# Grouped v weights, later decay exponentials, first tile by sequences, and a moved weight sum in a linear attention kernel with routed gate

## The chip, the cores and the metric

The kernel runs on one core of one Trainium2 chip. Times are device microseconds (us) of one execution. The kernel before took 1069.27 us (median of 3 runs, 1067.15 to 1069.29). Engines: PE = TensorE (matrix products), DVE = VectorE, ACT = ScalarE, POOL = GpSimd, SP = SyncE, which issues most DMAs; ACT issues some too.

## The reference

Input x has 4 sequences of 512 tokens and 512 features. With a layer norm, a linear attention of 16 heads of 128 with a decay for each head, and a gate that a router of 64 experts makes from their bias vectors:

```
xn = layernorm(x)
q, k, v = split(silu(xn @ w_qkv.T))                  # 16 heads of 128
o[t] = sum over s <= t of exp(-slope * (t - s)) * (q[t] . k[s]) * v[s]    # computed by blocks
o = norm_w * o * rsqrt(mean(o * o) + 1e-6)
s = (sigmoid(xn @ w_gate.T) * o) @ w_out.T
p, idx = top_k(softmax(xn @ router_w.T + router_b), 8)
g = silu(xn * sum(p) + sum over the 8 of p * expert_bias[idx])
out = x + s * g
```

## The kernel before, in words

**Products.** Every fp32 product is made of three fp32r passes: each operand is split into a high part, which ACT casts (split_hi, L100), and a low part, the rest, which DVE or POOL subtracts (split_lo, L103). Projections treat two sequences (a pair) as a 2x2 block matrix: the x blocks B11, T1, B21, B22 and the sums T2 to T4 on one side, the weight blocks A11, A12, A21, A22 and the sums S1 to S4 on the other. unit (L484) makes the result from 7 block products (PRODUCTS), each of 6 matmuls; plain_unit (L525) uses 8 and needs no sums. Each list after[i] in the code holds what is emitted after product i: work for other units, queued on its engine there.

**Stage v** (L939 to 1004). 16 units: for each of two groups of v weights (ws[0], ws[1]) the 8 tiles of 128 tokens x 2 sequences. The first two units (k = 0 and 1) are plain; in them DVE makes the four sums of the weights (sum_of, L421) and the S blocks are split, so that the third unit can use unit. Each unit also prepares a later tile: layer norm statistics (layer_norms, L221: DVE, with the power -1/2 on POOL, L232 or L236), normalising (L202, DVE), transposes (L251, PE) and their copy (L253, ACT), router logits (L318, PE), token sums (L268, POOL) and splits. Results go to DRAM (v<-vo_v, L588). A result's silu is a sigmoid on ACT (L555) and a product on DVE (L558), which is deferred to a later do_deferred; the product frees the PSUM bank. There are four such banks (ps_mm) and three of another pool (ps_sc), which transposes, logits and attention share.

**Start** (L892 to 937). SP issues x of the first two tiles and the eight pieces of the first v weights, each 128 rows of two runs of 1 KB (raw_v, L418). ACT's queue issues five small loads (L900 to 904). make_dist (POOL) and make_decays (ACT exponentials, then a memset on POOL, L169) build the decay rows. PE runs 32 transposes of the identity (warm_up, L150), then the first tile's transposes of both sequences, 6 more of the identity, logits and the first products.

**Decays.** keep_rows (L172) stores the 16 decay rows to DRAM; keep_decay(h) (L175) copies one row to 128 rows in DRAM, 16 DMAs on SP's queue in units 13 to 15 of stage v; load_decay (L655) reads it for head h. The router's exponentials (scores_exp, L337) run in unit 13, with a load of ACT's exponential table before and of the sigmoid's after.

**Head stage** (L1039 to 1095). For each of the two pairs 24 units: gates g and heads qk, three units to two heads. While a unit's products run, the attention of the head before it goes on PE: scores sa and transposed keys kt (scores_qk, L670), states ss, outputs o (attend, L707). The decay masks the scores on DVE (L680), which frees sa's bank of ps_sc; ACT scales the keys (L684) and POOL the queries (L686). y goes to DRAM.

**Output stage** (L1112 to 1155). For each sequence b and head h, o_head (L816) adds 12 matmuls into four banks. ahead(i, loads, splits) (L1015) loads y and w_o and splits them some heads ahead: y's low part on DVE, w_o's on POOL. The last unit of the head stage calls ahead in its after lists. The last head's attention is emitted in steps 0 to 2 of this stage. finish (L808) makes the result of a token tile and stores it, on SP's queue for the first three sequences.

Nothing reorders what is emitted: each engine works its instructions off in the order of the code, and a waiting one holds up those behind it.

Of the kernel before, what the change touches and what calls it, by code (L numbers as in the profile page):

```python
# [16 lines left out]
GH = 2  # L17
# [2 lines left out]
TOP_K = 8  # L20
LN_EPS = 1e-05
RMS_EPS = 1e-06
WARM = 32

# [24 lines left out]
def kernel(  # L51
# [44 lines left out]
    def tok(b, t):  # L96
        return bass.ds(b * N + t * P, P)

    def split_hi(hi, src):
        nc.scalar.copy(hi, src)  # L100

    def split_lo(eng, lo, src, hi):
        eng.tensor_tensor(lo, src, hi.bitcast(F32), ALU.subtract)  # L103
# [68 lines left out]
        nc.sync.dma_start(out=rows_d, in_=decay_row)  # L172

    def keep_decay(h):
        nc.sync.dma_start(out=decay_d[h], in_=rows_d[h : h + 1].to_broadcast([P, W]))  # L175


    stats = [const.tile([P, NT, 2], F32, tag=f"stats{b}", name=f"stats{b}") for b in range(B)]
# [39 lines left out]
        xts[b, t] = xt  # L218


    def layer_norms(p, t, apart=False):  # L221
        var = small.tile([P, PB], F32, tag="lnvar", name=f"lnv_{p}_{t}")
        for j in range(PB):
            b = p * PB + j
            st = small.tile([P, nc.vector.BN_STATS_DIM], F32, tag="bn", name=f"bn_{b}_{t}")
            nc.vector.bn_stats(st, xts[b, t])
            nc.vector.bn_aggr(stats[b][:, t, :], st)
            nc.vector.tensor_scalar(
                var[:, j : j + 1], stats[b][:, t, 1:2], 1.0, LN_EPS, ALU.mult, ALU.add
            )  # L230
            if apart:
                nc.gpsimd.tensor_tensor(  # L232
                    rstd_of[p][:, t, j : j + 1], var[:, j : j + 1], mhalf[:, 0:1], ALU.pow
                )
        if not apart:
            nc.gpsimd.tensor_tensor(rstd_of[p][:, t], var, mhalf[:, 0:PB], ALU.pow)  # L236

    def normalise_x(p, t):
        for b in range(p * PB, p * PB + PB):
# [94 lines left out]
            top = scores[p, "top"][:, :, None].to_broadcast([P, PB * NT, E])  # L334
            nc.vector.tensor_tensor(sc, sc, top, ALU.subtract)

    def scores_exp():  # L337
        for p in range(B // PB):
            nc.scalar.activation(scores[p], scores[p], AF.Exp)
        for b in range(B):  # L340
            nc.sync.dma_start(out=scores_d[b], in_=scores[b // PB][:, b % PB])

# [59 lines left out]
    class Weights:  # L402
# [38 lines left out]
            self.of[n] = self.wp.tile([P, 2, self.width], F32R, tag="w", name=f"w_{n}_{self.name}")  # L441


        def split_one(self, n, eng, piece=None, hi=False):
            src = self.sum[int(n[1]) - 1] if n[0] == "S" else self.raw[:, int(n[1]) - 1, int(n[2]) - 1]
            if n not in self.of:
                self.place(n)

            for i in (0, 1) if piece is None else (piece,):
                c = bass.ts(i, self.width // 2)  # L450
                if hi:
                    split_hi(self.of[n][:, 0, c], src[:, c])
                elif i == 0:
                    split_hi(self.of[n][:, 0], src)
                split_lo(eng, self.of[n][:, 1, c], src[:, c], self.of[n][:, 0, c])

        def splits(self, lo_engines):
            w, r, s, wp = self.width, self.raw, self.whole, self.wp
# [108 lines left out]

    def v_weights(p, g, rawp, sump, wp):
        def loads(raw):
            r = raw.rearrange("p i k (c w) -> p i k c w", c=KC)  # L570
            per = VH // GH
            return [
                (r[:, i, k, :, bass.ts(j, GH * P)], w_v[(2 * g + i) * per + j][:, bass.ts(k, KC)])
                for i in range(2) for k in range(2) for j in range(per)
            ]
        return Weights(f"v_{p}_{g}", KC * VW, rawp, sump, wp, loads, True)

    def v_unit(p, g, t, w, outp, after, direct=False):
        name = f"v_{p}_{g}_{t}"

        def operands(wn, xn, wi, xi, c):
            return blocks[p, xn][:, t, xi, c], w.of[wn][:, wi, bass.ts(c, VW)]

        def sink(i, j):
            dst = outp.tile([P, VW], F32, tag="vout", name=f"vo{i}{j}_{name}")

            def store():
                nc.sync.dma_start(out=v_d[p * PB + j, 2 * g + i][t], in_=dst)  # L588
            return dst, lambda src: silu_of(dst, src, f"{i}{j}_{name}", store)

        if direct:
            plain_unit(name, operands, lambda i, j, ps: sink(i, j)[1](ps), after)
            return
        unit(
            name, operands, lambda ps: sink(0, 0)[1](ps),
            [lambda: sink(1, 1), lambda: sink(0, 1), lambda: sink(1, 0)], after,
        )
# [202 lines left out]
    def split_wo(h, w):  # L800
# [3 lines left out]
        split_lo(nc.gpsimd, wr[:, 1], w, wr[:, 0])  # L804
        wos[h] = wr


    def finish(b, t, ps, c=slice(None)):  # L808
        u, xt = gates[b, t][:, c], xts[b, t][:, c]
        last = b == B - 1  # L810
        nc.vector.scalar_tensor_tensor(u, ps[:, c], rms[b][:, t : t + 1], u, ALU.mult, ALU.mult)  # L811
        (nc.vector if last else nc.gpsimd).tensor_tensor(u, u, xt, ALU.add)
        (nc.scalar if last and t % 2 else nc.sync).dma_start(out=out[tok(b, t), c], in_=u)


    def o_head(pos, h, yr, t, c=slice(None), stops=(NH - 1,)):  # L816
# [10 lines left out]
    NP_FIRST = 2  # L827

    def prepare(stage, p, t):
        first = (p, t) == (0, 0)  # L830

        def turn():
            for j in range(PB):
                transpose(stage, p, j, t)
            if p == 0:
                nc.sync.dma_start(out=xf_d[t], in_=xfs[p, t])

        if p == 0 and t < NP_FIRST:
            sums = (lambda: plain(p, t, nc.vector if t == 0 else nc.gpsimd)), lambda: None, lambda: None
        else:  # L840
            sums = combine(stage, p, t, nc.gpsimd)

        def route_logits():
            logits(stage, p, t)
        return {
            "stats": lambda: layer_norms(p, t, first), "norms": lambda: normalise_x(p, t),
            "turn": turn, "sums": sums[0], "plain": sums[1], "more": sums[2], "logits": route_logits,
        }

# [46 lines left out]
    vloads(4)  # L896
    make_first()

    nc.scalar.activation(kdecay[:, 0:NT], mhalf, AF.Exp)
    nc.scalar.dma_start(out=slope_of, in_=slope.rearrange("o h -> h o"))  # L900
    nc.scalar.dma_start(out=slopes, in_=slope.to_broadcast([P, NH]))
    nc.scalar.dma_start(out=rw, in_=router_w)
    nc.scalar.dma_start(out=rb, in_=router_b.to_broadcast([P, E]))
    nc.scalar.dma_start(out=nw, in_=norm_w)
    make_dist()
    sig = small.tile([P, NT], F32, tag="var", name="table")
    warm_up(WARM)
    for i, n in enumerate(XN):
        block(0, i, xa if i < NX else xb, i)
        blocks[1, n] = blocks[0, n]  # L910
    for n in ["A21"] + [n for n, _, _, _ in PRODUCTS]:
        ws[0].place(n)
    make_decays()

    nc.scalar.activation(sig, mhalf, AF.Sigmoid)
    prep[0]["stats"]()
    prep[0]["norms"]()

    pt = [transpose(stage, 0, j, 0, False) for j in range(PB)]
    nc.vector.tensor_copy(xfs[0, 0][:, 0], pt[0])  # L920
    b11, b12, b21, b22 = halves(xfs[0, 0])
    split_hi(blocks[0, "B11"][:, 0, 0], pt[0][:, 0:KC])
    ws[0].split_one("A11", nc.vector, hi=True)
    split_lo(nc.gpsimd, blocks[0, "B11"][:, 0, 1], b11, blocks[0, "B11"][:, 0, 0])
    nc.scalar.copy(xfs[0, 0][:, 1], pt[1])
    nc.sync.dma_start(out=xf_d[0], in_=xfs[0, 0])
    load_pair(stage, *tiles[2])
    warm_up(6)
    split_blocks(0, 0, nc.vector, (("T1", b12), ("B21", b21), ("B22", b22)))
    ws[0].split_one("A12", nc.vector, 0)  # L930
    ws[0].split_one("A12", nc.gpsimd, 1)
    logits(stage, 0, 0, [0])
    prep[1]["stats"]()
    prep[1]["norms"]()
    ws[0].split_one("A21", nc.vector)
# [3 lines left out]
    for k, (p, t) in enumerate(tiles + again):  # L939
# [20 lines left out]
        if k == 0:  # L960
            after[0].append(lambda: logits(stage, 0, 0, [1]))
        if k < NP_FIRST:
            for i in range(2 * k, 2 * k + 2):
                after[2 + 2 * (i % 2)].append(lambda i=i: ws[0].sum_of(i, nc.vector))
            for i, n in enumerate((("S1", "S2"), ("S3", "S4"))[k]):
                eng = nc.gpsimd if i else nc.vector
                after[2 * i + 3].append(lambda n=n, eng=eng: ws[0].split_one(n, eng))
        if k == NP_FIRST:
            after[0].append(ws[1].load())
        if n1 - 5 <= k < n1 - 1:  # L970
# [11 lines left out]
        if n1 < k <= n1 + NT:  # L982
            sums, split_plain, split_sums = combine(stage, 0, k - n1 - 1, nc.gpsimd, "r")
            after[1] += [sums, split_plain]
            after[4].append(split_sums)
        if k == NP_FIRST:
            after[0].append(keep_rows)
        if n1 + NT < k < n1 + 2 * NT:
            for j in range(1, len(PRODUCTS)):
                h = (k - n1 - NT - 1) * (len(PRODUCTS) - 1) + j - 1  # L990
                if h < NH:
                    after[j].append(lambda h=h: keep_decay(h))
        if k == n1 + NT + 1:
            after[1].append(scores_exp)
        if k == 2 * n1 - 2:
            vs_stack.close()
            todo = [(p, *u) for p in range(NP) for u in h_units(p, hw_stack)]
# [41 lines left out]
    for i, (p, kind, n, w) in enumerate(todo):  # L1039
# [5 lines left out]
            todo[i + 2][3].load()()  # L1045
        if i + 1 < len(todo):
            weight_steps(todo[i + 1][3], after)
        if pending is not None:
            for j, fs in enumerate(attention(*pending, attp)):
                after[j] += fs  # L1050
            if pending[1] == NH - 1:
                later.append(lambda: [sum_squares(b) for b in range(PB)])
            pending = None
# [20 lines left out]
        if i == len(todo) - 1:  # L1074
# [8 lines left out]
            after[3].append(more)  # L1083
            after[4].append(lambda: ahead(0, 4, 2))
            after[5].append(lambda: load_eb(op))
            after[6].append(lambda: ahead(0, 6, 3))
        if kind == "g":
            gate_unit(p, n, w, attp, after)
        else:
# [22 lines left out]
    for i, (b, h) in enumerate(steps):  # L1112
# [5 lines left out]

        if h < NH - 1:
            ahead(i, 6, 3)  # L1120
        if h == 0:
            for t in range(NT):
                pos[t] = ps_mm.tile([P, F], F32, tag="mm", name=f"po_{b}_{t}")
# [77 lines left out]
```

## Time and profile before

| | |
|---|---|
| runs | 1069.27 us median of 3 (1067.15 to 1069.29) |
| the profiled execution | 1068.67 us, of which the span from first to last instruction is 1066.9 |
| mean granted clock of PE | 0.997 |
| first product of stage v | 9.73 us |
| stage v ends, head stage begins on PE | 187.73 us |
| first matmuls of the output stage | 865.74 us |
| the last matmuls start | 1061.67 us |
| DMA | 143.11 MB, 134 GB/s over the span |

A timeline line reads: start in us, time in us, engine, line of the code, operation, result<-operands, partitions x elements, how many; in brackets the idle time of the engine before it and what ended it. SPq and ACTq are DMA issues. A waits line reads: engine, what waited, its line <- what released it: total us, times, longest. A wait is put down to what came last by the profile.

### The profile page before, as it was taken

The page shows a single profiled execution, that of the slowest core. Times are in us where ns is not written, and L with a number is a line of the kernel's source. Part 1 is how long each engine was busy: PE and PEld are TensorE (multiplying, and loading weights), DVE is VectorE, ACT ScalarE, POOL GpSimd, SP SyncE. Part 2 cuts the span into 40 slices and gives each one's busy share as a digit, 9 for nine tenths or more (in the row PEclk, how much of TensorE's full clock was granted, in tenths as well). Part 3 has the DMA queues.
Part 4 walks back from the last instruction along what each step waited for, and adds up shares of the span by engine and source line. Part 5 has one row for each costly group of instructions (what it writes and reads, how often), then busy time and mean ns, then how long its engine had stood idle before and what let it go on. Part 6 is the DMA issues. An engine that isn't in the chain of part 4 may idle for free.

```text
span 1066.9 us, 16491 instructions
## 1 busy us (share of the span) xinstructions
PE 1056.2 (99%) x5771; PEld 910.9 (85%) x5771; DVE 695.6 (65%) x1061; ACT 476.1 (45%) x923; POOL 727.3 (68%) x710
## 2 busy tenths in 40 slices
PE   9999999999999999999999999999999989999998
PEld 8888788888888888888888888888888878888886
DVE  7898876667576666665756756657567556754464
ACT  5555554544444444444444444444444434332321
POOL 5898892868787678777785787777867847612130
PEclk9999999999999999999999999999999999999999
DMA  6557747522423333235722232232222436354351
GB/s 224 184 177 251 262 145 235 160 84 88 136 84 94 103 97 108 75 124 195 254 84 83 87 115 78 85 128 84 84 91 90 149 109 206 119 178 168 98 194 53
DMA packets 109875, 143.11 MB, mean 134 GB/s; under 512 B 9680, under 2 KB 58208, under 8 KB 108896
## 3 DMA queue, kind: packets, MB, share of 16 engines
q1 hardware_dynamic: 108752, 141.35, 40.7%
q8 instruction: 46, 0.75, 0.3%
q10 hardware_dynamic: 1040, 0.71, 0.2%
q14 instruction: 37, 0.30, 0.1%
HBM read 93.24 MB, written 50.87 MB: 135 GB/s over the span
## 4 chain that ended last, share of the span: by engine, by line
PE 93%; DVE 3%; DMA 2%; POOL 1%; SPq 1%; issue 1%; ACT 1%; DVEq 0%; ACTq 0%
PE u_qk L502 28%; PE po L818 16%; PE u_g L502 14%; PE u_v L502 11%; PE sa L675 5%; PE o L712 5%; PE ss L698 4%; PE o L714 4%; PE kt L678 2%; DMA raw_v<-in_w_v_dram 1%; PE lg L318 1%; PE pu L769 1%; DMA v<-vo_v 1%; DVE k L558 1%; POOL ts L268 0%
## 5 line engine op out<-in xcount | busy, mean ns | idle before, releaser
L818 PE MATMUL po<-wr,yr 128*128 128x512 f32 (+1 forms) x777 | 179.5, 389 | 1.0 <-DVE u L811 1.0
L818 PEld LDWEIGHTS po<-wr,yr 128*128 128x128 f32 x777 | 144.5, 188 | 31.2 <-DVE u L811 1.2
L502 PE MATMUL u_qk<-blk_T,ws_qk 128*128 128x512 f32 x576 | 147.1, 395 | 0.0
L724 POOL TENSOR_TENSOR sqs<-sqs,sq 128x512 f32<-128x512 f32 x60 | 78.5, 1309 | 78.3 <-ACT sq L723 78.3
L502 PEld LDWEIGHTS u_qk<-blk_T,ws_qk 128*128 128x128 f32 x576 | 105.7, 188 | 20.5
L103 DVE TENSOR_TENSOR yr<-yin,yr 128x512 fp32r<-128x512 f32 x64 | 71.5, 1127 | 50.1 <-ACT yr L100 50.0
L103 POOL TENSOR_TENSOR ws_qk<-sum_qk,ws_qk 128x512 fp32r<-128x512 f32 x64 | 82.8, 1295 | 30.7 <-ACT ws_qk L100 29.9
L502 PE MATMUL u_qk<-blk_B,wa_qk 128*128 128x512 f32 x384 | 99.1, 393 | 0.0
L558 DVE TENSOR_TENSOR k<-k,sg_k 128x512 f32<-128x512 f32 x64 | 92.3, 1442 | 2.4 <-ACT sg_k L555 2.2
L712 PE MATMUL o<-at,vin 128*128 128x128 f32 x512 | 88.4, 275 | 0.0
L502 PEld LDWEIGHTS u_qk<-blk_B,wa_qk 128*128 128x128 f32 x384 | 70.9, 188 | 14.2
L702 DVE SCALAR_TENSOR_TENSOR st<-st,bdecay,ss 128x128 f32<-128x128 f32 x128 | 41.7, 346 | 61.4 <-ACT st L700 59.1
L555 ACT ACTIVATE sg_k<-k 128x512 f32<-128x512 f32 x64 | 40.5, 632 | 86.6 <-DVE k L493 86.6
L712 PEld LDWEIGHTS o<-at,vin 128*128 128x128 f32 x512 | 74.9, 191 | 2.5
L502 PE MATMUL u_g<-blk_T,ws_g 128*128 128x512 f32 x288 | 76.0, 399 | 0.0
L714 PE MATMUL o<-qd,st 128*128 128x128 f32 x384 | 74.2, 275 | 0.0
L103 POOL TENSOR_TENSOR ws_g<-sum_g,ws_g 128x512 fp32r<-128x512 f32 x32 | 42.7, 1334 | 44.7 <-ACT ws_g L100 44.7
L675 PE MATMUL sa<-q,k 128*128 128x128 f32 x512 | 68.7, 278 | 3.2 <-DVE k L558 3.2
L675 PEld LDWEIGHTS sa<-q,k 128*128 128x128 f32 x512 | 65.1, 193 | 6.6 <-issue 3.2
L777 POOL TENSOR_TENSOR u<-u,sgu 128x512 f32<-128x512 f32 x16 | 20.7, 1292 | 70.1 <-ACT sgu L776 57.4
L716 DVE SCALAR_TENSOR_TENSOR y<-o,nw,gt 128x512 f32<-128x512 f32 x64 | 47.6, 747 | 31.7 <-PE o L714 30.1
L723 ACT ACTIVATE sq<-o 128x512 f32<-128x512 f32 x60 | 35.9, 598 | 71.4 <-POOL sqs L724 43.1
(186 smaller groups left out, 2420.5 us busy)
## 6 DMA issues: line engine op xcount, KB each, us to landing
v<-vo_v SPq DMA_DIRECT2D x64, 256.0 KB, 2.1
raw_qk<-in_w_head_dram SPq DMA_DIRECT2D x64, 256.0 KB, 3.6
vin<-v SPq DMA_DIRECT2D x64, 256.0 KB, 3.6
y<-y SPq DMA_DIRECT2D x64, 256.0 KB, 2.0
yin<-y SPq DMA_DIRECT2D x64, 256.0 KB, 3.0
x<-in_x_dram SPq DMA_DIRECT2D x32, 256.0 KB, 4.3
raw_g<-in_w_head_dram SPq DMA_DIRECT2D x32, 256.0 KB, 3.2
raw_v<-in_w_v_dram SPq DMA_DIRECT2D x16, 256.0 KB, 5.6
```

The source lines that it names most:

```text
L103: eng.tensor_tensor(lo, src, hi.bitcast(F32), ALU.subtract)
L502: nc.tensor.matmul(ps, lhsT, rhs, start=(first and c == 0 and n == 0), stop=(c == KC - 1 and n == len(PASSES) - 1), skip_group_check=not f ...
L555: nc.scalar.activation(sg, src, AF.Sigmoid)
L558: nc.vector.tensor_tensor(dst, src, sg, ALU.mult)
L675: nc.tensor.matmul(pa[:, c], k[:, c], q[:, c], start=True, stop=True)
L698: nc.tensor.matmul(ps[:, c], kd[s][:, c], v_of(b, h, c), start=True, stop=True)
L702: nc.vector.scalar_tensor_tensor(r[:, c], r[:, c - 1], bdecay[:, h : h + 1], ps[:, c], ALU.mult, ALU.add)
L712: nc.tensor.matmul(o, v_of(b, h, c), at[s][:, c], start=True, stop=(c == 0))
L714: nc.tensor.matmul(o, st[s][:, c - 1], qd[s][:, c - 1], start=False, stop=True)
L716: nc.vector.scalar_tensor_tensor(y, po, nw[:, h : h + 1], gts[s], ALU.mult, ALU.mult)
L724: nc.gpsimd.tensor_tensor(sq[b], sq[b], s1, ALU.add)
L818: nc.tensor.matmul(pos[t][:, c], yr[:, yi, bass.ts(t, P)], wos[h][:, wi, c], start=(h == 0 and n == 0), stop=(h in stops and n == len(PASS ...
```

## The change

- The raw weights of v are laid out by groups of two heads: a piece is 128 rows of one run of 2 KB. Matmuls and splits read them through piece, in two runs of 256; ACT's high parts of a whole block stay in one run. For the first block, A11, high and low parts are made for each half of the contraction (hi_of, lo_of).
- The exponentials of the decays move to the router's, in unit 13, and the rows' store there. The DMAs of keep_decay go to ACT's queue: three in each of units 14 and 15, the other ten in the first ten units of the head stage. ACT's first table load is the sigmoid's; make_dist moves behind the first tile's second transposes; the small loads change their order.
- The first tile goes by sequences: statistics, normalising and transposes of sequence 0, then of sequence 1, with splits of A11 between. 26 warm-ups in place of 32; the other six stand behind the first transposes. The copy of the first transposes moves from DVE to ACT.
- The fourth weight sum and its split move from the second unit to the third (k = 2), behind its first product.
- The last unit of the head stage splits two heads of y ahead and not three; the third is split in step 0 of the output stage, behind do_deferred.
- Stores of the first three sequences' results are kept in a list and issued behind the next step's loads.

```diff
-WARM = 32
+WARM = 26
...
     def keep_decay(h):
-        nc.sync.dma_start(out=decay_d[h], in_=rows_d[h : h + 1].to_broadcast([P, W]))
+        nc.scalar.dma_start(out=decay_d[h], in_=rows_d[h : h + 1].to_broadcast([P, W]))
...
-    def layer_norms(p, t, apart=False):
+    def layer_norms(p, t, js=range(PB)):
...
-        for j in range(PB):
+        for j in js:
...
+        c = slice(js[0], js[-1] + 1)
+        nc.gpsimd.tensor_tensor(rstd_of[p][:, t, c], var[:, c], mhalf[:, c], ALU.pow)
...
-    def scores_exp():
+    def exponentials():
         for p in range(B // PB):
             nc.scalar.activation(scores[p], scores[p], AF.Exp)
+        make_decays()
...
+        def piece(self, a, c):
+            return a.rearrange("p (j c w) -> p c j w", c=KC, w=GH * P)[:, c]
...
+        def hi_of(self, n, c):
+            src = self.source(n)
+            split_hi(self.piece(self.of[n][:, 0], c), self.piece(src, c))
+
+        def lo_of(self, n, c, eng):
+            hi, lo = (self.piece(self.of[n][:, i], c) for i in range(2))
+            split_lo(eng, lo, self.piece(self.source(n), c), hi)
...
         def loads(raw):
-            r = raw.rearrange("p i k (c w) -> p i k c w", c=KC)
             per = VH // GH
+            r = raw.rearrange("p i k (j c w) -> p i k j c w", j=per, c=KC)
             return [
-                (r[:, i, k, :, bass.ts(j, GH * P)], w_v[(2 * g + i) * per + j][:, bass.ts(k, KC)])
+                (r[:, i, k, j], w_v[(2 * g + i) * per + j][:, bass.ts(k, KC)])
...
-            return blocks[p, xn][:, t, xi, c], w.of[wn][:, wi, bass.ts(c, VW)]
+            return blocks[p, xn][:, t, xi, c], w.piece(w.of[wn][:, wi], c)
...
+        def store():
+            (nc.scalar if last and t % 2 else nc.sync).dma_start(out=out[tok(b, t), c], in_=u)
+        if last:
+            store()
+        else:
+            stores.append(store)
...
-    nc.scalar.activation(kdecay[:, 0:NT], mhalf, AF.Exp)
-    nc.scalar.dma_start(out=slope_of, in_=slope.rearrange("o h -> h o"))
-    nc.scalar.dma_start(out=slopes, in_=slope.to_broadcast([P, NH]))
+    table = small.tile([P, NT], F32, tag="var", name="table")
+    nc.scalar.activation(table, mhalf, AF.Sigmoid)
     nc.scalar.dma_start(out=rw, in_=router_w)
     nc.scalar.dma_start(out=rb, in_=router_b.to_broadcast([P, E]))
     nc.scalar.dma_start(out=nw, in_=norm_w)
-    make_dist()
-    sig = small.tile([P, NT], F32, tag="var", name="table")
+    nc.scalar.dma_start(out=slope_of, in_=slope.rearrange("o h -> h o"))
+    nc.scalar.dma_start(out=slopes, in_=slope.to_broadcast([P, NH]))
     warm_up(WARM)
...
-    make_decays()
-
-    nc.scalar.activation(sig, mhalf, AF.Sigmoid)
-    prep[0]["stats"]()
-    prep[0]["norms"]()
-
-    pt = [transpose(stage, 0, j, 0, False) for j in range(PB)]
-    nc.vector.tensor_copy(xfs[0, 0][:, 0], pt[0])
+
+    layer_norms(0, 0, [0])
+    normalise(xts[0, 0], xts[0, 0], 0, 0)
+    pt = transpose(stage, 0, 0, 0, False)
+    warm_up(6)
+    layer_norms(0, 0, [1])
+    ws[0].hi_of("A11", 0)
+    split_hi(blocks[0, "B11"][:, 0, 0], pt[:, 0:KC])
+    nc.scalar.copy(xfs[0, 0][:, 0], pt)
     b11, b12, b21, b22 = halves(xfs[0, 0])
-    split_hi(blocks[0, "B11"][:, 0, 0], pt[0][:, 0:KC])
-    ws[0].split_one("A11", nc.vector, hi=True)
+    ws[0].hi_of("A11", 1)
+    ws[0].lo_of("A11", 0, nc.vector)
+    normalise(xts[1, 0], xts[1, 0], 1, 0)
+    logits(stage, 0, 0, [0])
     split_lo(nc.gpsimd, blocks[0, "B11"][:, 0, 1], b11, blocks[0, "B11"][:, 0, 0])
-    nc.scalar.copy(xfs[0, 0][:, 1], pt[1])
+    ws[0].lo_of("A11", 1, nc.vector)
+    transpose(stage, 0, 1, 0)
+    make_dist()
...
-    warm_up(6)
...
-    logits(stage, 0, 0, [0])
...
         if k < NP_FIRST:
-            for i in range(2 * k, 2 * k + 2):
+            for i in range(2 * k, 2 * k + 2 - k):
                 after[2 + 2 * (i % 2)].append(lambda i=i: ws[0].sum_of(i, nc.vector))
-            for i, n in enumerate((("S1", "S2"), ("S3", "S4"))[k]):
+            for i, n in enumerate((("S1", "S2"), ("S3",))[k]):
                 eng = nc.gpsimd if i else nc.vector
                 after[2 * i + 3].append(lambda n=n, eng=eng: ws[0].split_one(n, eng))
+        if k == NP_FIRST:
+            after[0] += [lambda: ws[0].sum_of(3, nc.vector), lambda: ws[0].split_one("S4", nc.gpsimd)]
...
-        if k == NP_FIRST:
-            after[0].append(keep_rows)
-        if n1 + NT < k < n1 + 2 * NT:
-            for j in range(1, len(PRODUCTS)):
-                h = (k - n1 - NT - 1) * (len(PRODUCTS) - 1) + j - 1
-                if h < NH:
-                    after[j].append(lambda h=h: keep_decay(h))
+        if k > n1 + NT + 1:
+            for j in (2, 4, 6):
+                after[j].append(lambda h=3 * (k - n1 - NT - 2) + j // 2 - 1: keep_decay(h))
         if k == n1 + NT + 1:
-            after[1].append(scores_exp)
+            after[1] += [exponentials, keep_rows]
...
+        if 6 + i < NH:
+            after[2].append(lambda i=i: keep_decay(6 + i))
...
-            after[6].append(lambda: ahead(0, 6, 3))
+            after[6].append(lambda: ahead(0, 6, 2))
...
         if h < NH - 1:
             ahead(i, 6, 3)
+            while stores:
+                stores.pop(0)()
```

More of the change, by code (lines that the diff above doesn't have):

```diff
@@ L230, in layer_norms @@
             )
[L231 to L236, printed above, removed]
+        c = slice(js[0], js[-1] + 1)
+        nc.gpsimd.tensor_tensor(rstd_of[p][:, t, c], var[:, c], mhalf[:, c], ALU.pow)
     def normalise_x(p, t):
@@ L441, in place, with source, split_one @@
             self.of[n] = self.wp.tile([P, 2, self.width], F32R, tag="w", name=f"w_{n}_{self.name}")
-        def split_one(self, n, eng, piece=None, hi=False):
-            src = self.sum[int(n[1]) - 1] if n[0] == "S" else self.raw[:, int(n[1]) - 1, int(n[2]) - 1]
+        def piece(self, a, c):
+            return a.rearrange("p (j c w) -> p c j w", c=KC, w=GH * P)[:, c]
+        def source(self, n):
             if n not in self.of:
                 self.place(n)
[L449 to L453, printed above, removed]
+            return self.sum[int(n[1]) - 1] if n[0] == "S" else self.raw[:, int(n[1]) - 1, int(n[2]) - 1]
+        def hi_of(self, n, c):
[4 more added lines that the diff above has]
+            split_lo(eng, lo, self.piece(self.source(n), c), hi)
+        def split_one(self, n, eng, c=None):
+            for i in range(KC) if c is None else (c,):
+                if i == 0:
+                    src = self.source(n)
                     split_hi(self.of[n][:, 0], src)
-                split_lo(eng, self.of[n][:, 1, c], src[:, c], self.of[n][:, 0, c])
+                self.lo_of(n, i, eng)
         def splits(self, lo_engines):
@@ L805, in split_wo @@
         wos[h] = wr
+    stores = []
     def finish(b, t, ps, c=slice(None)):
@@ L812, in finish @@
         (nc.vector if last else nc.gpsimd).tensor_tensor(u, u, xt, ALU.add)
-        (nc.scalar if last and t % 2 else nc.sync).dma_start(out=out[tok(b, t), c], in_=u)
+        def store():
[4 more added lines that the diff above has]
+            stores.append(store)
     def o_head(pos, h, yr, t, c=slice(None), stops=(NH - 1,)):
@@ L829, in prepare @@
     def prepare(stage, p, t):
-        first = (p, t) == (0, 0)
         def turn():
@@ L845, in prepare @@
         return {
-            "stats": lambda: layer_norms(p, t, first), "norms": lambda: normalise_x(p, t),
+            "stats": lambda: layer_norms(p, t), "norms": lambda: normalise_x(p, t),
             "turn": turn, "sums": sums[0], "plain": sums[1], "more": sums[2], "logits": route_logits,
```

## The prediction

> **What bounds the kernel now.** I read the page's busy table first, then its chain, then what TensorE (PE) waited for, then the timelines of the stretches that those waits point to.
>
> ```profile
> PE 1056.2 (99%) x5771; PEld 910.9 (85%) x5771; DVE 695.6 (65%) x1061; ACT 476.1 (45%) x923; POOL 727.3 (68%) x710
> ...
> PE 93%; DVE 3%; DMA 2%; POOL 1%; SPq 1%; issue 1%; ACT 1%; DVEq 0%; ACTq 0%
> ```
>
> PE holds 93% of the chain and its work does not change: the same products, in nearly the same order. What can be won lies in the 10.7 us in which PE is not busy, and in stretches where it is slow. The waits of PE over the whole span are only these four:
>
> ```profile
> PE sa L675 <- DVE k L558: 3.2, 2, 3.0
> PE warm L150 <- POOL ident masks.py:199: 1.4, 1, 1.4
> PE u_v L502 <- DVE vo_v L558: 1.0, 1, 1.0
> PE po L818 <- DVE u L811: 1.0, 1, 1.0
> ```
>
> The second and fourth are the start and the end, which the change leaves. The first is at 870 us, the third at 42 us; the change touches the cause of both. So I take it place by place.
>
> **The last unit (ahead(0, 6, 2)).** VectorE's (DVE's) timeline there:
>
> ```profile
> 865.81 1.40 DVE L716 SCALAR_TENSOR_TENSOR y<-o,nw,gt 128x512 f32<-128x512 f32 x2
> 869.73 1.36 DVE L103 TENSOR_TENSOR yr<-yin,yr 128x512 fp32r<-128x512 f32 x1 [2.52 <-ACT yr L100]
> 871.01 1.75 DVE L558 TENSOR_TENSOR k<-k,sg_k 128x512 f32<-128x512 f32 x1
> 872.68 0.68 DVE L680 TENSOR_TENSOR at<-sa,dec 128x512 f32<-128x512 f32 x1
> ```
>
> The third split of y stands ahead of the last k product in DVE's queue and waits 2.52 us for ScalarE's (ACT's) cast, which itself waits behind two squares that GpSimd (POOL) serialises. PE waits for that k: its first keys' transposes end at about 869.9 and the second scores start at 872.91, 2.96 us idle. The clock then halves:
>
> ```profile
> 873.00:874.00 1.00, 1.00 (x5) 1.00 (x6) 0.36 (x1) 0.00 (x0) 1.00 (x2) 0.50 0.78 242
> ```
>
> (A stretch of 1 us: busy time of PE, its weight loads, DVE, ACT and POOL, then the granted clock, 0.50; in the stretch from 876 it is back at 0.87.) From the first score matmul at 868.56 to the states at 878.58 it takes 10.02 us. With the third split moved behind do_deferred, k follows y directly at 867.2; even at 1.75 us it ends at 868.95, before PE needs it. At full clock 8 score matmuls take 0.89, three transposes 0.33, 12 output matmuls 12 x 0.227 = 2.72. Scores, transposes and scores end at 868.56 + 0.89 + 0.33 + 0.89 = 870.67. What is late next: the last transposes need the PSUM buffer that the first scores hold (three buffers), freed by the mask at L680, which now stands behind the split of y: 869.73 + 1.36 + 0.68 = 871.8. PE waits 1.1 us there, then 0.33 + 2.72, states at 874.85: **3.7 us won**. Bounds: 4.9 if nothing waits (873.7), 2.0 if the 1.1 us wait costs the clock again (half clock from 872.9 to 876.1 cost 0.95 + 0.31 + 0.47 on the three groups that it met, 1.7). I take 3.7: at 42 us PE waits 1.0 and the groups after it keep their pace. ACT's order there is unchanged, and POOL's low part of the third weight, behind it, is needed only two heads later.
>
> **The fourth weight sum.** Today at the second unit's end:
>
> ```profile
> 41.13 1.56 DVE L438 TENSOR_TENSOR sum_v<-raw_v,sum_v 128x1024 f32<-128x1024 f32 x1
> ...
> 42.61 1.28 DVE L558 TENSOR_TENSOR vo_v<-d_v,sg_v 128x512 f32<-128x512 f32 x2
> ...
> 43.34 1.65 PE L502 MATMUL u_v<-w_S_v,blk_T 128*128 128x512 f32 x6 [1.00 <-DVE vo_v L558]
> ...
> 43.93 2.55 POOL L103 TENSOR_TENSOR w_S_v<-sum_v,w_S_v 128x512 fp32r<-128x512 f32 x2
> ```
>
> PE's third product needs a PSUM bank whose product (L558) stands behind the sum. Without the sum it frees at 41.9; PE goes on at 42.06, 1.28 us sooner. But the sum now follows both products, at 42.6 to 43.85, its cast ends at 44.9 and POOL starts the low part at 44.95 and not at 43.93, 1.0 later. POOL is full here (9.84 us of the ten from 50). Everything behind the low part is 1.0 later: the token sums, rstd and the splits of tile 3. Its four T splits take POOL from 52.45 to 56.7; the first ends now at 53.5, PE uses it at 54.5 (second matmul of the fourth unit's second product, 54.28 + 0.23): 1.0 slack, which PE's lead of 1.28 and POOL's delay of 1.0 to 1.3 use up. PE stalls in the fourth unit until POOL is there: +0.0 to +0.3, I take **+0.2**, against -1.28 if POOL were free. POOL has slack again in the fifth unit (1.12 idle at 68.66).
>
> **The first tile.** Today:
>
> ```profile
> 5.77 0.19 POOL L169 MEMSET decay_row<- 16x127 f32 x1 [3.17 <-ACT decay_row L166]
> 5.94 1.19 POOL L232 TENSOR_TENSOR rstd<-lnv,mhalf 128x1 f32<-128x1 f32 x2
> ...
> 8.57 0.37 ACT L100 CAST blk_B<-pt 128x256 fp32r<-128x256 f32 x1 [1.05 <-DVE xf L920]
> 8.84 1.14 ACT L100 CAST w_A_v<-raw_v 128x512 fp32r<-128x512 f32 x2
> ```
>
> Moving the decays takes away the memset that holds POOL's first power until 5.94: it can run at 4.78, x is normalised by 5.97 and transposed from about 6.1, 1.05 earlier than 7.15. Six fewer warm-ups (about 0.16 us each, 1.0 in all) end just there. One table load (1.28) and three decay activations (1.0) leave ACT while it idles, worth nothing. But ACT's first work is now the high part of A11's first half, and that needs two raw pieces; the second lands at 7.9 today (issued near 2.1, 5.8 to landing). Call its new landing T. Then, by start-to-start steps of 0.52 (512 wide) and 0.30 (256 wide): B11 at T+0.5, copy T+0.8 to T+1.4, logits (0.80) to T+2.25, second transposes and their copy T+2.95 to T+3.55, three casts, A12's cast at T+4.5, against 11.42 today: T - 6.9. Pieces of 2 KB in place of 1 KB: the trace shows 380 GB/s for raw_v alone near 7.2, up to 414 at 16 to 17, where x's 2 KB rows take part. T lies between 6.25 (then the transposes' result at 6.8 decides) and 7.9. I take 7.5: +0.6. Behind it DVE's chain (statistics, normalise, A21) has 0.38 of slack before the first v product at 18.84, so the stage moves by +0.2, bounds -1.1 to +0.6. Later raw pieces land earlier (today 14 to 17), which only removes a wait that this chain covers.
>
> PE may stand idle from about 7.2 to T + 1.45 = 8.95, 1.75 us, between the 1.0 that left the clock and the 2.96 that halved it; half clock would double the logits and transposes (1.2 us).
> The Trainium skill ("TensorE: Matmul & The Clock Gate", Part 4: PE-mode transpose) says that transposes do not count as busy for the clock. Here the warm-ups, all transposes, go from 6 or 7 a us to 12 a us at about 6.0, so the trace disagrees; by the page the six warm-ups in the gap would not hold the clock and the sum would get 1.2 us worse, by the row nothing.
>
> **Decays and stores.** Sixteen broadcasts leave SP's queue for ACT's. Today they crowd a v store:
>
> ```profile
> 173.76 6.56 DMA v<-vo_v
> ```
>
> which costs PE 0.2 us at 182.35. **-0.2.** On ACT an issue takes 0.34 to 0.45, and once one came 2.07 late (nw, 2.70 to 4.77): 0 to 2.1 us each. Queued behind is the next sigmoid, before which ACT idles 2.1 on average in the qk units (68.0 us in 32); its product frees a bank used a unit later. So 0, at worst +0.5. The first broadcast waits for the rows' store, issued near 165.5; today that took 5.8, 171.3, when ACT reaches it at about 171 and idles to 174.18. The exponentials lengthen ACT's table stretch at 162.7 by 1.0, and the sigmoid behind ends at about 166.8, when DVE wants it (166.63).
> The Trainium skill ("Perfetto Trace Analysis", DMA Instruction — HWDGE (DVE, Sync)) says that one descriptor generator is locked by one sequencer at a time, which speaks against a second queue; no row here separates that from other causes of the 2.07, and either way my sum keeps 0.
> Deferred stores let SP's loads of y pass 5 us earlier, but PE lost only 0.3 at that boundary, to DVE: 0.
>
> **Sum** against the profiled execution: -3.7 + 0.2 + 0.2 - 0.2 = -3.5. It took 1068.67 us (span 1066.9 and 1.8 around it), 0.6 under the median 1069.27, within the runs shown. 1068.67 - 3.5 = **1065.2**.
>
> **Rivals.** (1) Forecast, 1065.2, chance 0.52, own range 1064.0 to 1066.4. The announced gain at 42 us does not arrive in it. (2) It arrives: POOL's delay is hidden, or T is near 6.3. Then -1.28 or -1.1 stands in place of +0.2: 1068.67 - 3.7 - 0.2 - 1.3 = 1063.5, chance 0.20. For it: POOL's splits took 4.7 where 3.96 is possible. Against: POOL is full from 29.7 to 67. (3) The last unit trades one wait for another: the 1.1 us at the PSUM buffer halves the clock again, 2.0 won and not 3.7: 1066.9, chance 0.22; up to 1068.5 with the start at its worst bounds (+0.6, +0.3, and 1.2 for the clock). (4) Slower: v's weights are now read as two runs of 256 by 14 x 42 + 2 x 48 = 684 matmuls. At e ns each this decides from 8 ns (684 x 0.008 = 5.5, more than 3.5 + 2.1); at 10 ns 1072.0. Against it: qk's moving operand is four runs of 128 and keeps 54 matmuls in 12.24 us, 0.227 each, as v does. Chance 0.06.
>
> The range 1062.4 to 1068.5 reaches from (2) with the end at its full 4.9 (1062.3) to the worst of (3). A measurement of this kernel can tell about 0.2%, 2.1 us. Faster by more: (1), (2) and a little of (3) that stays under 1066.5, 0.74; same 0.20; slower 0.06.
>
> **What would show it.** In the new profile: no PE wait on k, but one of about 1 us before the last transposes, clock 1.00 around 872; no wait at 42, but a later one on POOL's T split near 52 to 55; first transposes near 6.1, A12's cast near 12; 684 v matmuls at 0.227. I am wrong if the second raw piece lands far from 7.5, if the last transposes do not share the first scores' buffer, or if ACT's queue is held by its DMAs for longer than its idle time.

## The result and the profile after

The kernel after took 1067.44 us (median of 14 runs, 1064.67 to 1068.96), beside 1068.41 for the kernel before (14 runs, 1067.1 to 1070.49): ratio 0.9987, 95% interval 0.9978 to 0.9996. So it is about 1 us faster, where 3.5 was forecast. The profiled execution took 1067.51 us (span 1065.7). The busy table and the shares of its chain:

```profile
PE 1054.1 (99%) x5765; PEld 909.1 (85%) x5765; DVE 698.4 (66%) x1060; ACT 475.4 (45%) x922; POOL 727.9 (68%) x710
...
PE 91%; DVE 4%; POOL 1%; DMA 1%; issue 1%; ACT 1%; SPq 0%; DVEq 0%; ACTq 0%; POOLq 0%
```

PE still sets the end. What it waited for over the whole span (total us, times, longest; left out are the start, 1.4, and two waits of 0.2):

```profile
...
PE kt L687 <- DVE at L689: 1.3, 1, 1.3
PE d_v L543 <- DVE w_A_v L103: 1.2, 2, 0.7
PE lg L314 <- ACT xf L935: 1.1, 1, 1.1
PE po L835 <- DVE u L822: 1.0, 1, 1.0
PE u_v L511 <- POOL blk_B L103: 0.6, 1, 0.6
PE u_v L511 <- DVE a_v L502: 0.6, 1, 0.6
```

The wait of 3.0 us for k and that of 1.0 us for the product near 42 us are gone. Of the new waits the first (masks, last unit), the third (first tile) and the fifth (GpSimd, fourth unit) had been forecast. The second, in the first unit's weight splits, had not. The last, at 119 us, is there in some executions and not in others of the same stage-v code (it is missing in experiment 8). It stands in six of the nine profiled executions of kernels built on the kernel after, and in none of the four of kernels built on the kernel before (the latter are the kernel before and experiments 3, 4 and 9); what it hangs on stays open. Stretch by stretch, after minus before, by the starts of the same PE groups in the two profiled executions:

| stretch | before | after | difference |
|---|---|---|---|
| start to first product | 9.73 | 10.33 | +0.60 |
| start to third unit | 38.55 | 41.13 | +2.58 |
| start to first output matmuls | 865.74 | 868.28 | +2.54 |
| from there to the last head's states | 12.84 | 9.55 | -3.29 |
| from there to the last matmuls | 183.09 | 182.70 | -0.39 |

So the last unit gave almost what was forecast, and the first 40 us gave most of it back. Last unit, timeline of PE and DVE in the kernel after:

```profile
868.36 1.40 DVE L725 SCALAR_TENSOR_TENSOR y<-o,nw,gt 128x512 f32<-128x512 f32 x2
869.68 0.68 DVE L567 TENSOR_TENSOR k<-k,sg_k 128x512 f32<-128x512 f32 x1
...
872.67 1.36 DVE L103 TENSOR_TENSOR yr<-yin,yr 128x512 fp32r<-128x512 f32 x1 [2.32 <-ACT yr L100]
873.96 1.27 DVE L689 TENSOR_TENSOR at<-sa,dec 128x512 f32<-128x512 f32 x2
...
874.69 0.55 PE L687 MATMUL kt<-ident,k 128*128 128x128 f32 x3 [1.32 <-DVE at L689]
```

The k product follows y at once; the split of y now stands before the masks, and PE waits 1.32 us before the last transposes. In the stretches of 1 us there the granted clock stays 1.00:

```profile
874.00:875.00 1.00, 0.31 (x4) 0.31 (x4) 1.00 (x3) 0.00 (x0) 1.00 (x1) 1.00 0.69 256
```

And the first unit's splits of A21 (DVE) and A22 (POOL), in the kernel after:

```profile
17.40 3.22 POOL L103 TENSOR_TENSOR w_A_v<-raw_v,w_A_v 128x512 fp32r<-128x512 f32 x2 [0.66 <-ACT w_A_v L100]
...
17.70 3.47 DVE L103 TENSOR_TENSOR w_A_v<-raw_v,w_A_v 128x512 fp32r<-128x512 f32 x2
...
19.53 0.97 PE L543 MATMUL d_v<-w_A_v,blk_B 128*128 128x512 f32 x3 [0.50 <-DVE w_A_v L103]
21.22 0.50 PE L543 MATMUL d_v<-w_A_v,blk_B 128*128 128x512 f32 x1 [0.72 <-DVE w_A_v L103]
```

The same lines in the kernel before:

```profile
16.96 1.29 DVE L103 TENSOR_TENSOR w_A_v<-raw_v,w_A_v 128x512 fp32r<-128x512 f32 x2
...
18.39 2.55 POOL L103 TENSOR_TENSOR w_A_v<-raw_v,w_A_v 128x512 fp32r<-128x512 f32 x2 [2.40 <-ACT w_A_v L100]
```

In the kernel before POOL came 0.14 us after DVE had ended, and a half took 0.65 us on DVE and 1.28 on POOL. In the kernel after POOL came 0.30 us ahead of DVE, and DVE's two halves took 3.47. In this execution the sizes fit turns taken one at a time: from 17.40, POOL 1.28, DVE 0.65, POOL 1.28, DVE 0.65 ends POOL at 20.61 and DVE at 21.26; measured 20.62 and 21.17. The Trainium skill ("SBUF — State Buffer", Who interferes with whom) says that a DVE instruction with two SBUF inputs and a GpSimd instruction that reads SBUF share a read port, and that whichever starts first holds it for its whole instruction. These rows agree with it. Strict turns are no rule, though: where DVE came first, both of its halves ran before POOL's first (experiment 8).

### The profile page after: what moved, and what is told of

It is laid out like the page before. It is cut to its first block, busy times and chain, and to the rows that moved or that the text cites. A ratio compares the mean times of both kernels' runs of the same rounds, so it can differ in the third digit from the quotient of the medians.

```text
span 1065.7 us, 16474 instructions
## 1 busy us (share of the span) xinstructions
PE 1054.1 (99%) x5765; PEld 909.1 (85%) x5765; DVE 698.4 (66%) x1060; ACT 475.4 (45%) x922; POOL 727.9 (68%) x710
## 4 chain that ended last, share of the span: by engine, by line
PE 91%; DVE 4%; POOL 1%; DMA 1%; issue 1%; ACT 1%; SPq 0%; DVEq 0%; ACTq 0%; POOLq 0%
PE u_qk L511 28%; PE po L835 16%; PE u_g L511 14%; PE u_v L511 10%; PE o L721 5%; PE sa L684 5%; PE ss L707 4%; PE o L723 4%; PE kt L687 2%; DMA raw_v<-in_w_v_dram 1%; PE pu L778 1%; PE lg L314 1%; POOL ts L264 1%; DVE w_A_v L103 1%; DVE vo_v L567 1%
## 5 line engine op out<-in xcount | busy, mean ns | idle before, releaser
L786 POOL TENSOR_TENSOR u<-u,sgu 128x512 f32<-128x512 f32 x16 | 20.7, 1291 | 69.7 <-ACT sgu L785 60.0
```

## The experiments

Each was run in 5 rounds beside the kernel before (the last in 3). Theory: the stage's loss is this collision, which the later first tile triggers; the rest of the change does what the prediction says. Main rival: the first tile's lateness itself, carried through the chain.

**1. A22's split later.** The kernel after, with POOL's split of A22 emitted behind the first unit's second product, so that DVE's split of A21 always comes first:

```diff
-    ws[0].split_one("A22", nc.gpsimd)
...
             after[0].append(lambda: logits(stage, 0, 0, [1]))
+            after[1].insert(0, lambda: ws[0].split_one("A22", nc.gpsimd))
```

> The changed kernel with the split of A22 emitted behind the first unit's second pair of products and not before the first unit. Theory (collision): in the changed kernel A22's low part on POOL (17.4 to 20.6) runs beside A21's low part on DVE, whose two halves take 1.7 us each instead of 0.65, and this holds the whole stage v. Then A21's halves take about 0.7 each here, the third unit starts on PE about 1.5 us sooner than 41.13, and the time falls from 1067.4 to about 1066.0. Rival (late first tile): A12's cast, 0.7 later than before, sets the stage; then nothing moves by more than 0.3.

Measured 1064.89 us (1064.75 to 1065.59), ratio 0.9971 (0.9959 to 0.9982), 0.0016 or 1.7 us below the kernel after. All six runs lie below all but one of the fourteen of the kernel after. The two splits in this kernel:

```profile
17.76 1.29 DVE L103 TENSOR_TENSOR w_A_v<-raw_v,w_A_v 128x512 fp32r<-128x512 f32 x2
...
18.93 2.55 POOL L103 TENSOR_TENSOR w_A_v<-raw_v,w_A_v 128x512 fp32r<-128x512 f32 x2 [2.13 <-ACT w_A_v L100]
```

DVE starts as late as in the kernel after (17.76), but its halves are back at 0.65. The third unit starts at 39.36, 1.77 before the kernel after, and only 0.8 behind the kernel before. The collision is shown. The lateness that remains, 0.8 here, is more than the forecast's +0.2 and its bound of +0.6.

**2. The old first tile.** The kernel after with the first tile's order of the kernel before (both sequences' transposes together, 32 warm-ups, A11's parts behind them), keeping the moved decay exponentials and all else:

```diff
-WARM = 26
+WARM = 32
...
-    layer_norms(0, 0, [0])
-    normalise(xts[0, 0], xts[0, 0], 0, 0)
-    pt = transpose(stage, 0, 0, 0, False)
...
+    layer_norms(0, 0, [0])
+    layer_norms(0, 0, [1])
+    prep[0]["norms"]()
+    pt = [transpose(stage, 0, j, 0, False) for j in range(PB)]
```

> The changed kernel with the first tile in the order of before (both sequences together, 32 warm-ups, first copy on DVE), all else as changed. Theory (collision): A22's raw piece still lands at about 16, POOL's split of A22 still runs beside DVE's split of A21, so at most 0.7 us of the 2.5 that stage v lost come back: about 1066.8. Rival (late first tile): the whole 2.5 come back, 1065.0.

Measured 1064.58 us (1063.69 to 1066.44), ratio 0.9968 (0.9957 to 0.998). The expectation under the theory was wrong, since it took the collision to stay with the earlier DVE. It goes:

```profile
16.71 1.29 DVE L103 TENSOR_TENSOR w_A_v<-raw_v,w_A_v 128x512 fp32r<-128x512 f32 x2
...
17.62 2.77 POOL L103 TENSOR_TENSOR w_A_v<-raw_v,w_A_v 128x512 fp32r<-128x512 f32 x2 [1.87 <-ACT w_A_v L100]
```

DVE is 0.99 earlier than in the kernel after and comes first; POOL, 0.91 behind it, loses only its first 0.2 us. So the new first tile is the trigger and the collision the cost. Experiments 1 and 2 differ by the lateness and by the place of A22's split: 0.3 us of median, inside both spreads. In their profiled executions the third unit starts 1.05 us apart (39.36 and 38.31), and the first output matmuls still 1.22 (866.40 and 865.18). There the lateness is carried through, as the rival says, beside the collision; what it is worth in the median stays open.

**3. Only the moved split of y.** The kernel before with one line changed:

```diff
-            after[6].append(lambda: ahead(0, 6, 3))
+            after[6].append(lambda: ahead(0, 6, 2))
```

> The kernel before with one edit, two splits of y ahead in the last unit of the head stage and not three. Theory: the 10.02 us from the last head's first scores to its states become 6.7 and the rest follows one to one: 1068.4 - 3.3 = 1065.1. Rival: the output stage's splits and loads are late instead and give back about 2 us: 1067.

Measured 1065.2 us (1064.1 to 1068.16), ratio 0.9973 (0.9963 to 0.9982): -3.1 us by the medians (1068.27 beside it). From the first output matmuls to the states it takes 9.54 us (864.88 to 874.42), as in the kernel after. This one line is worth more than the whole change.

**4. Only the fourth sum moved.** The kernel before with the sum and its split in the third unit, as in the change.

```diff
-            for i in range(2 * k, 2 * k + 2):
+            for i in range(2 * k, 2 * k + 2 - k):
...
-            for i, n in enumerate((("S1", "S2"), ("S3", "S4"))[k]):
+            for i, n in enumerate((("S1", "S2"), ("S3",))[k]):
...
+            after[0] += [lambda: ws[0].sum_of(3, nc.vector), lambda: ws[0].split_one("S4", nc.gpsimd)]
```

> The kernel before with one edit, the fourth weight sum and its split in the third unit. Theory (POOL-bound): PE's wait of 1.0 at 42 us goes, POOL's low part of S4 starts 1.0 later and PE waits for POOL in the fourth unit, near 52 to 55; time 1068.2 to 1068.6, no change. Rival: the 1.28 us arrive, 1067.1.

Measured 1068.52 us (1066.34 to 1071.18), ratio 1.0002 (0.9991 to 1.0014). The wait at 42 us is gone, a wait of 0.26 us for POOL at 51.40 has come. In the kernel after the same chain reads, on POOL and PE:

```profile
47.58 2.52 POOL L103 TENSOR_TENSOR w_S_v<-sum_v,w_S_v 128x512 fp32r<-128x512 f32 x2 [2.24 <-ACT w_S_v L100]
...
54.40 1.43 PE L511 MATMUL u_v<-w_A_v,blk_B 128*128 128x512 f32 x5 [0.61 <-POOL blk_B L103]
```

POOL idles 2.24 us for its operand, and PE pays for it in the fourth unit. Counted from the start of the third unit, its fourth product comes 1.29 us sooner in experiment 4 than in the profiled execution of before (4.99 and 6.28), and the fourth unit's logits 0.59 sooner (20.70 and 21.29). But the wait at 42 us is not always 1.0: in experiments 3 and 9, with the sum in its old place, it was 0.4, and there the same logits come at 20.7 too.

**5. The fourth sum early.** Experiment 1 with the sum moved the other way, right behind the third sum in the second unit:

```diff
-            for i in range(2 * k, 2 * k + 2 - k):
-                after[2 + 2 * (i % 2)].append(lambda i=i: ws[0].sum_of(i, nc.vector))
+            for i in range(2 * k, 2 * k + 2):
+                after[2 if k else 2 + 2 * (i % 2)].append(lambda i=i: ws[0].sum_of(i, nc.vector))
...
-            after[0] += [lambda: ws[0].sum_of(3, nc.vector), lambda: ws[0].split_one("S4", nc.gpsimd)]
+            after[0].append(lambda: ws[0].split_one("S4", nc.gpsimd))
```

> The kernel after, with GpSimd's low part of A22 emitted behind VectorE's of A21 (as in the first experiment, 1064.9 us) and the fourth sum made in the second unit right behind the third, only its split staying in the third unit. If the fourth sum gains little because GpSimd gets its operand late (2.25 us idle before S4's low part), that idle time goes, the fourth unit's wait of 0.29 us for GpSimd goes, and the time is 0.3 us below the first experiment: 1064.6. Rival: the sum again delays the product that frees a PSUM bank, TensorE waits up to 1 us near 42 us as in the kernel before, and the time is 1065.3 to 1065.9.

Measured 1064.62 us (1063.93 to 1065.71), ratio 0.9962 (0.9949 to 0.9975). PE's wait for POOL near 52 us is gone, the wait at 42 us does not return, and the fourth unit's logits start at 59.47, 0.61 before experiment 1. The 0.3 us of median are too small to be shown by the times.

**6. The third split of y behind step 0.** The kernel after with:

```diff
-            ahead(i, 6, 3)
+            ahead(i, 6, 3 if i else 2)
...
             for f in last_steps[i]:
                 f()
+            if i == 0:
+                ahead(0, 6, 3)
```

> The kernel after, but the third split of y is emitted behind the whole of step 0 of the output stage, so that the mask that frees the PSUM bank of the first scores does not stand behind it. If the 1.32 us wait before the last transposes comes from that place in VectorE's queue, it goes: the first mask at about 872.1 and not 873.96, transposes at 873.4, time 1.3 us less than the kernel after, 1066.1 to 1066.3 by the same ratio to the kernel before. Rival: the key scaling on ScalarE or the mask's own wait for the scores is late next, and less than 0.5 us is won.

Measured 1065.67 us (1065.02 to 1067.05), ratio 0.9975 (0.9965 to 0.9986), 0.0012 or 1.3 us below the kernel after. From first output matmuls to states it takes 8.01 us in place of 9.55, with no wait of PE for the masks. In its profiled execution the splits met in a third way. A22 had landed early, POOL split it from 16.48, and DVE's normalising was held:

```profile
16.53 2.90 DVE L202 TENSOR_SCALAR x<-x,stats,rstd 128x512 f32<-128x512 f32 x2 [0.83 <-POOL rstd L232]
```

(1.00 us for the two in the kernel after.) The third unit started at 40.95, as late as in the kernel after.

**7. The three together.** The old first tile of experiment 2, the early sum of 5, the split of 6.

> The kernel after with the first tile as in the kernel before (second experiment, 1064.6 us), the fourth sum made in the second unit, and the third split of y behind step 0. If the three terms add up: 1064.6 - 1.3 (wait before the last transposes) - 0.3 (GpSimd's low part of S4 earlier) = 1063.0 us, faster than every kernel so far. Rival: the last unit's wait moves on, and the sum's old wait returns near 42 us: 1064.6 to 1065.0.

Measured 1062.14 us (1061.59 to 1064.09), ratio 0.9942 (0.9925 to 0.996): the fastest kernel of this study, with three waits of PE left, the first two of which are start and end:

```profile
PE warm L150 <- POOL ones L143: 1.4, 1, 1.4
PE po L835 <- DVE u L822: 1.0, 1, 1.0
PE sa L684 <- DVE k L567: 0.2, 1, 0.2
```

**8. Stores at once.** The kernel after with `store()` called in finish for every sequence:

```diff
-        if last:
-            store()
-        else:
-            stores.append(store)
+        store()
```

> The kernel after, with the result stores of the first three sequences issued at once, as in the kernel before. If the 0.4 us that the trace shows at the three sequence boundaries (0.12, 0.16 and 0.12 us) comes from the deferred stores, these come back and the time is 0.4 us more than that of the kernel after. Rival, as forecast: the stores are worth nothing, no difference beyond 0.1 us at the boundaries.

Measured 1067.48 us (1064.4 to 1068.36), ratio 0.9986 (0.9974 to 0.9998): no difference. From the gate matmuls (L778) of the first sequence to those of the fourth, across the three boundaries, it takes 129.84 us here and 129.85 in the kernel after. The 0.4 us by which the kernel before was slower there (130.25) are scatter: other executions show 129.84 to 130.78. The forecast of 0 was right and my reading of the trace wrong. The profiled execution shows something else. It took 1064.40, with the very start that cost the kernel after 2 us:

```profile
17.50 3.78 POOL L103 TENSOR_TENSOR w_A_v<-raw_v,w_A_v 128x512 fp32r<-128x512 f32 x2 [0.87 <-ACT w_A_v L100]
...
17.58 1.28 DVE L103 TENSOR_TENSOR w_A_v<-raw_v,w_A_v 128x512 fp32r<-128x512 f32 x2
```

Here DVE came first with both of its halves (17.58 to 18.86) and POOL was held (2.53 and 1.29 us a half), and the third unit started at 39.22. The last raw pieces land at another time in each execution (A21's cast starts between 13.7 and 15.2 in the nine profiled ones with the new layout, between 14.8 and 15.9 in the four with the old), so the same code runs into the collision in one execution and not in the next. Of the 26 runs of the kernel after and this one, three took 1064.4 to 1065.3 us and the others 1066.7 or more.

**9. Lateness alone, on the kernel before.**

```diff
+    idle = small.tile([P, nc.vector.BN_STATS_DIM], F32, tag="bn", name="idle")
+    nc.vector.bn_stats(idle, xts[0, 0])
     prep[1]["stats"]()
```

> The kernel before with nothing of the change, but one more statistics instruction of 0.69 us on VectorE ahead of tile 1's statistics: it makes VectorE's split of A21 as late as the new first tile does, with nothing else of it. If whichever of VectorE and GpSimd starts first holds the other up, GpSimd's split of A22 now comes first in most executions: third unit 1.5 to 2.5 us later than 38.55 us, median of the kernel +1.2 to +2.5 us; VectorE's halves of A21 (or its normalising) take 1.4 us or more in place of 0.65. Rival: lateness alone counts, 0.69 less the slack of 0.38: third unit at 38.9, median +0.3 us, each half 0.65 us.

Measured 1069.52 us (1068.43 to 1071.85), ratio 1.0015 (1.0005 to 1.0024), +1.5 us by the medians (1067.99 beside it). The size is the theory's, but the profiled execution, 1069.44, is no witness for it. DVE (17.87) and POOL (17.85) met within 0.02 us, DVE came first with 0.65 a half, and the third unit started at 39.52. Of that 0.97 us later, 0.28 was left at the first output matmuls. Whether the median comes from collisions in other executions stays open.

**10. The fastest kernel with A22's split late as well.** Experiment 7 plus the edit of experiment 1.

> The fastest kernel so far (1062.1 us: first tile as before, fourth sum in the second unit, third split of y behind step 0) with GpSimd's split of A22 emitted behind VectorE's of A21 as well. With the old first tile VectorE came first in each trace, so nothing is won in the median: 1061.8 to 1062.5 us. Rival: the two splits collide in some of its executions too, and the median falls by over 0.5 us.

Measured 1062.52 us (1062.22 to 1063.17), ratio 0.9953 (0.994 to 0.9965): no gain, as expected. With the old first tile DVE came first in the profiled executions anyhow.

**11. The decay DMAs on SP's queue.** Experiment 5 with:

```diff
-        nc.scalar.dma_start(out=decay_d[h], in_=rows_d[h : h + 1].to_broadcast([P, W]))
+        nc.sync.dma_start(out=decay_d[h], in_=rows_d[h : h + 1].to_broadcast([P, W]))
```

> The kernel of 1064.6 us (the kernel after with A22's split later and the fourth sum in the second unit), with the sixteen decay broadcasts issued on SP's queue again and not on ScalarE's. Forecast: SP's queue holds up a v store for once, TensorE waits 0.2 us near 180 us and the time is 0.2 us more. Rival: on SP they cost nothing at these places, the time is the same within 0.2 us and the trace shows no new wait of TensorE in the last v units.

Measured 1064.89 us (1064.13 to 1065.23), ratio 0.9966 (0.9956 to 0.9976), beside 1064.62 in experiment 5. That is the forecast's +0.2 in size, but no run separates it from nothing, and the trace shows no wait of PE between 70 and 200 us: the rival holds at these places.

## Why the prediction was right and wrong, point by point

- **The last unit: -3.7 forecast, -3.29 in the trace, -3.1 alone (experiment 3).** Mechanism and place were right: k directly behind y, the next wait at the masks, the clock not lowered by it. The wait there was 1.32 us and not 1.1. Rival 3, the clock halved again, did not come.
- **The fourth sum: +0.2 forecast.** +0.25 by the medians alone (experiment 4), not to be told from 0. The gain of 1.28 us did arrive at 42 us, and a little over half of it was given back in the fourth unit, as argued, though at B's split (53.62 in the kernel after) and not at T's. The rest is no gain beside experiments 3 and 9, where the wait at 42 us was 0.4: the forecast read its 1.0 from one execution. Rival 2 falls.
- **The first tile: +0.2 forecast, +2.54 found at the first output matmuls.** T was taken as 7.5, and A11's first cast started at 7.60. A12's cast came 0.74 later (forecast +0.6). The arithmetic held that far; the first transposes came at 6.66 and not near 6.1, which cost nothing, since A11's cast waited for its raw piece. What failed is the next step: "Later raw pieces land earlier (today 14 to 17), which only removes a wait that this chain covers." The chain on DVE does cover a wait of its own, but POOL's split of A22 also starts at the landing of a raw piece. With DVE 0.74 later and A22's cast 0.99 earlier (17.26 to 16.27), POOL came ahead of DVE. DVE's A21, on the path, took 3.47 us in place of 1.29: +2.2, and +1.8 at the third unit by experiment 1. The bound of +0.6 knew only starts; it took every duration as fixed. The lateness was undersized too: without the collision the third unit still started 0.7 to 0.8 late (39.22 in experiment 8, 39.36 in experiment 1), where +0.2 was forecast. That the pieces land earlier because of the change is not shown: with the old layout A21's cast started at 14.79, 14.95, 15.33 and 15.88 in four executions, with the new one between 13.74 and 15.23 in nine.
- **It could have been seen.** The trace of before has the same instruction with and without POOL beside it: DVE's halves of A21 at 0.65, and those of S3 beside POOL's four T splits nearly twice that:

```profile
38.65 2.36 DVE L103 TENSOR_TENSOR w_S_v<-sum_v,w_S_v 128x512 fp32r<-128x512 f32 x2
...
39.28 4.69 POOL L103 TENSOR_TENSOR blk_T<-ts,blk_T 128x256 fp32r<-128x256 f32 x4
```

- **Decays and stores.** -0.2 is neither shown nor excluded; 0 for the stores held (experiment 8). The issue that the forecast saw 2.07 late (nw, 2.70 to 4.77) was no price of ACT's queue. In the trace of before it waits for the semaphore of x's second DMA, which it uses again; the last landing on that semaphore stands at 4.74. The row behind it on ACT names the same DMA:

```profile
5.21 0.51 ACT L166 ACTIVATE decay_row<-decay_row,rest_of 16x256 f32<-16x256 f32 x1 [2.99 <-DMA x<-in_x_dram]
```

- **Strided v weights (rival 4).** In the kernel after, six v matmuls take 1.36 us from start to start (111.68 to 113.04), 0.227 each, the price that the forecast read from before. No cost.
- **The sum.** -3.3 (last unit) + 2.5 (first 40 us) - 0.4 (scatter in the output stage) = -1.2, the difference of the two spans. The forecast of -3.5 was out by about 2.4 us, nearly all of it from the first tile: by experiment 1 about 1.8 from the collision, the rest from the lateness. The time lies inside the range given, but outside the forecast's own (1064.0 to 1066.4); the range reached there for the clock of rival 3, which did not come, so that it lies inside is luck.

## What to carry to other kernels

When a change moves one engine's chain by under 1 us, look at what the other engines start on a landing DMA or a semaphore nearby, and ask whether the order in time turns over: a duration is only good for the neighbours it was measured with. Where DVE and POOL both read two SBUF tensors, let the one on the path start first by the order of the code, not by luck. And take a many-part change apart on the chip: here one line held more than the whole gain.

## What the runs showed of the hardware

- The same fp32 subtraction of 128x512 took DVE 0.65 us alone and 1.77 when POOL's subtraction had started 0.30 us before it; POOL's took 1.28 alone and 2.53 when DVE was first with two of them. Normalising (one SBUF tensor and values per partition) took 1.00 us for two alone and 2.90 beside POOL. Where the recorded starts lay within 0.1 us, DVE came first twice, though POOL's record was the earlier.
- PE's clock was halved after 2.96 us without work in the kernel before; after 1.32 us (874.69) and after 1.11 us (9.03) in the kernel after it stayed at 1.00.
